# Where a selective scan takes its decay, its start state and its gate: four edits to one stage of a four-layer network

## The chip, the cores and the metric

The kernel runs on one core of a Trainium2 chip. The metric is device time in microseconds (us) for one execution of the whole program; three runs of the kernel before gave 5123.48, 5127.48 and 5133.85, median 5127.48 us. The engines are named as the profile names them: PE (matmuls), DVE (the vector engine), ACT (the scalar engine), POOL (GpSimd) and SP, whose queue issues nearly all DMAs. Each works through its own list of instructions in order, and semaphores make one wait for another. PSUM has eight banks of 128x512 f32 here, handed out by one pool.

## The reference, cut to what matters

Four layers of attention-like and feed-forward blocks run one after the other on a batch of 2. The change touches only the mixer of the third layer, a selective scan with 2048 channels and 16 states each over a sequence of 1024 (the kernel takes it over `S = 1024` as two halves of 512):

```python
def step(h, inp):
    x_t, dt_t, B_t, C_t = inp
    dA = jnp.exp(dt_t[..., None] * A)
    dBx = dt_t[..., None] * B_t[:, None, :] * x_t[..., None]
    h = dA * h + dBx
    y = jnp.einsum('bdn,bn->bd', h, C_t)
    return (h, y)
...
dt = jax.nn.softplus(dt + dt_bias[None, :, None])
...
y = (ys + D_param[None, :, None] * xc) * jax.nn.silu(z)
```

So each of 2048 x 16 rows needs a decay `dA` (an exponential), a term `dBx`, a recurrence along time, a product with `C`, a sum over the 16 states and a gate `silu(z)`.

## The kernel before, in words

`l2_attn` runs this stage once for each of the two batch entries. In it a loop over **slots** k does the scans; its order is written by hand (`manual_schedule`), so each engine's list is the order in which the loop emits. There are `SL = 128` slots for each half of the sequence (u = 0, then u = 1), so 256 a batch entry and 512 in all. Eight slots make a **chunk** of 128 channels; a slot holds 16 channels with 16 states, as two tiles (m = 0, 1) of 128 rows by 512 time steps.

What a slot k emits, in this order:

- `rows(k + 6)`: one DMA from DRAM (`dxd`) that spreads dt times x of the slot's channels over the states, into a tile `h` (nine buffers, 512 KB).
- `times_b(k + 2)`: POOL multiplies `h` by B (L1279, 128x1024).
- `keep(k - 1)`: in the first half only, ACT saves the last state of each row into `hst` in SBUF (L1304).
- `pe()`: one of two "calls", matmuls of other work that PE does alongside (input projections, gates, output projections of the first half).
- for m = 0 and 1: `scan(k, m)` on DVE (L1296; it reads the decay from PSUM and `h`, and writes `h`), then `decay(k + 1, m)`: a matmul on PE that spreads dt over the states into a PSUM bank (L1286), and ACT's exponential in place (L1288). In the second half ACT then adds the state carried over from the first half: `h[:, 0] += dA[:, 0] * hst`, a 128x1 operation (L1291); `scan` itself always starts from 0.0.
- between the two m: what has been put off to this slot with `at(...)`, and a second call.
- `states` in odd slots: matmuls that sum h times C over the states into a PSUM bank `py` (L1318; the first of a chunk is L1316).
- `times_c(k - 1)`: DVE multiplies `h` by C (L1307, 128x1024).

So DVE's own work in a plain slot is two scans and one L1307. Beside these stand, in the first half, three L1124 for each of 16 chunks (the conv's taps) and, in the second, additions to x and statistics (L152, L163).

**dt's chain.** `l2_dt` is called 16 slots before a chunk's first slot (call that slot k) and puts off the steps of softplus: relu, abs and exp on ACT at k+1 (`act1`), three more ACT operations at k+2 (`act2`, the last ones L1226 to L1228), two POOL operations at k+3 (`pool1`, L1231 and L1232), the sum at k+4 (L1235), dt times x at k+5 (`times_x`, L1238) with four DMAs to `dxd` (L1240), a rounded copy `hl` on ACT and its low part `lo` on POOL at k+7 (L1247, L1252), and two DMAs `hl<-lo` at k+8 (`send`, L1258). x itself (`xi`) is loaded at k+3. The chunk's `rows` begin at k+10, its decays at k+15. Tiles `e`, `one`, `lg` and `rl` have one buffer each.

**The gate.** `y_out` is put off to 8 slots after the chunk's fifth slot: ACT copies `py` from PSUM to a tile `one` (L1332), POOL multiplies the gate `zt` by it (L1333), SP writes the product to DRAM (L1334). `zt` holds silu(z), which `silu_z` makes in pairs on ACT, with a table load ahead and one behind (at L1129 and L193).

After the loop the second half's output projection reads these products back (`out_proj`, L1618 and L1622).

Of the kernel before, what the change touches and what calls it, by code (L numbers as in the profile page):

```python
# [11 lines left out]
AF = mybir.ActivationFunctionType  # L12
ALU = mybir.AluOpType
# [14 lines left out]
class Net:  # L28
# [1032 lines left out]
    def l2_attn(self, b, ready, last):  # L1061
        nc, i = self.nc, self.i
        NCH, N, NR = 16, 16, 64
        NF = NR + 2 * N
        SL = 8 * NCH
        with (
# [24 lines left out]
            hst = lp.tile([P, NCH * N], F, name=self.nm("hst"))  # L1091

            def tmp(tag, bufs=2, n=HALF):
                return tp.tile([P, n], F, tag=tag, bufs=bufs, name=self.nm(tag))
# [4 lines left out]
            xcd, yd = [dram(t, [P, HALF]) for t in ("xcd", "yd")]  # L1099
# [3 lines left out]
            px, norms, hl, hs, dA, py, xs = {}, {}, {}, {}, {}, {}, {}  # L1103
# [6 lines left out]
            def at(k, f, *args):  # L1110
                late.setdefault(k, []).append((f, args))
# [96 lines left out]
            def l2_dt(u, c, k):  # L1208

                p = self.ps()  # L1210
                nc.tensor.matmul(
                    p, wd[c // 8][: NF + 1, (c % 8) * P : (c % 8 + 1) * P], norms[u][0], start=True, stop=True
                )
                xs[u, c] = xc = tmp("xi")
                at(k + 3, nc.sync.dma_start, xc, xcd[u][c][:])
                e, one, lg = tmp("e", 1), tmp("one", 1), tmp("lg", 1)
                dt, dtx = lg, e
                rl = tmp("rl", 1)

                def act1():  # L1220
                    nc.scalar.activation(rl, p, AF.Relu)
                    nc.scalar.activation(e, p, AF.Abs)
                    nc.scalar.activation(e, e, AF.Exp, scale=-1.0)

                def act2():
                    nc.scalar.activation(one, e, AF.Identity, bias=self.one)  # L1226
                    nc.scalar.activation(lg, one, AF.Ln)
                    nc.scalar.activation(one, one, AF.Identity, bias=neg)  # L1228

                def pool1():  # L1230
                    nc.gpsimd.tensor_tensor(e, e, one, ALU.subtract)  # L1231
                    nc.gpsimd.tensor_tensor(lg, lg, e, ALU.add)  # L1232

                def sum1():
                    nc.gpsimd.tensor_tensor(dt, lg, rl, ALU.add)  # L1235

                def times_x():
                    nc.gpsimd.tensor_tensor(dtx, dt, xc, ALU.mult)  # L1238
                    for j in range(4):
                        nc.sync.dma_start(dxd[u][c][:, j, :], dtx[32 * j : 32 * j + 32, :])  # L1240

                low = [None]

                def parts():

                    hl[u, c] = tp.tile([P, 2, HALF], R, tag="hl", bufs=2, name=self.nm("hl"))
                    nc.scalar.copy(hl[u, c], dt.unsqueeze(1).to_broadcast([P, 2, HALF]))  # L1247

                def rest():

                    lo = low[0] = tp.tile([P, HALF], R, tag="lo", bufs=1, name=self.nm("lo"))
                    nc.gpsimd.tensor_tensor(lo, dt, hl[u, c][:, 0, :].bitcast(F), ALU.subtract)  # L1252

                def send():

                    lo = low[0]
                    for j in range(2):
                        nc.sync.dma_start(  # L1258
                            hl[u, c][64 - 64 * j : P - 64 * j, j, :].bitcast(F), lo[64 * j : 64 * j + 64, :].bitcast(F)
                        )  # L1260

                for n, f in ((1, act1), (2, act2), (3, pool1), (4, sum1), (5, times_x), (7, parts), (7, rest), (8, send)):
                    at(k + n, f)


# [17 lines left out]
            def decay(k, m):  # L1283
                u, c, q, jj = of(k)
                dA[k, m] = self.ps()
                nc.tensor.matmul(dA[k, m], rep[:, 4 * m + q, :], hl[u, c][:, jj, :], start=True, stop=True)  # L1286
                g = 16 * c + 4 * q + 2 * jj + m
                nc.scalar.activation(dA[k, m], dA[k, m], AF.Exp, scale=A[:, g : g + 1])  # L1288
                if u:
                    h0 = hs[k][:, m, 0:1]  # L1290
                    nc.scalar.activation(h0, dA[k, m][:, 0:1], AF.Identity, scale=hst[:, g : g + 1], bias=h0)  # L1291

            def scan(k, m):
                u, c, q, jj = of(k)
                g = 16 * c + 4 * q + 2 * jj + m
                nc.vector.tensor_tensor_scan(  # L1296
                    hs[k][:, m, :], dA.pop((k, m)), hs[k][:, m, :], 0.0, ALU.mult, ALU.add
                )

            def keep(k):  # L1300
# [27 lines left out]
            def y_out(k):  # L1328
                u, c = k // SL, k % SL // 8
                sz = zt.pop((u, c))  # L1330
                yo = tmp("one", 1)
                nc.scalar.copy(yo, py.pop((u, c)))  # L1332
                nc.gpsimd.tensor_tensor(sz, sz, yo, ALU.mult)  # L1333
                nc.sync.dma_start(yd[u][c][:], sz)  # L1334

            def ins(u):
# [125 lines left out]
            with self.tc.manual_schedule():  # L1462

                todo, ahead = [], []

                def take(units, lead):
                    for n, (load, calls) in enumerate(units):
                        ahead.append((len(todo) - lead, load))
                        todo.extend(calls)

                z0, z1, x1 = gates(0), gates(1), ins(1)
                take(z0[:2] + x1[:6], 20)
                for n in range(2, 12, 2):
                    take(z0[n : n + 2] + x1[n + 4 : n + 6], 20)
                take(xproj(1), 4)
                take(z0[12:] + z1[:6], 20)
                taken = 0
                at(-BEFORE, lambda: at(4 - BEFORE, l2_spread, 0, l2_norm(0)))
                for k in range(-BEFORE, 2 * SL + 6):
                    if -16 <= k < 2 * SL - 16 and k % 8 == 0:  # L1480
                        l2_dt((k + 16) // SL, (k + 16) % SL // 8, k)
                    if k == SL + 12:
                        o = outs(0)
                        for n, (a, z) in enumerate(((6, 10), (10, 12), (12, 16), (16, 16))):
                            take(o[8 * n : 8 * n + 8], 8)
                            take(z1[a:z], 20)
                    if k == -1 or k == SL:
                        l2_cr(max(k, 0) // SL)
                    n = 3 if k < -1 else 2
                    batch = []  # L1490
                    for _ in range(n):
                        while ahead and ahead[0][0] <= taken:
                            ahead.pop(0)[1]()
                        if taken < len(todo):
                            batch.append(todo[taken])
                            taken += 1

                    def pe(last=False):
                        while batch and (last or len(batch) > n - 1):
                            f, *args = batch.pop(0)  # L1500
                            if f:
                                f(*args, k)

                    live = 0 <= k < 2 * SL
                    if 0 <= k + 6 < 2 * SL:
                        rows(k + 6)
                    if 0 <= k + 2 < 2 * SL:
                        times_b(k + 2)
                    if 0 <= k - 1 < 2 * SL:
                        keep(k - 1)  # L1510
                    pe()
                    for m in range(2):
                        if live:
                            scan(k, m)
                        if 0 <= k + 1 < 2 * SL:
                            decay(k + 1, m)
                        if m:
                            break
                        for f, args in late.pop(k, []):
                            f(*args)  # L1520
                        pe(True)
                    if k % 2 == 1 and 0 <= k - 2 < 2 * SL:
                        states(k - 2)
                    if 0 <= k - 1 < 2 * SL:
                        times_c(k - 1)
                    if live and k % 8 == 4:
                        at(k + 8, y_out, k)
                    if live and k % 8 == 0:
                        skip(k // SL, k % SL // 8)
                while late:  # L1530
                    for f, args in late.pop(min(late)):
                        f(*args)
# [460 lines left out]
```

## Time and profile before

| | |
|---|---|
| three runs, median | 5127.48 us (5123.48 to 5133.85) |
| the profiled execution, its own time | 5130.32 us |
| its span in the profile | 5128.4 us |
| granted TensorE clock, mean | 0.968 |
| scan loop, first batch entry | 1052 to 2006 us |
| scan loop, second batch entry | 3602 to 4548 us |
| L1296, the scans | 1024 of 1207 ns mean |
| L1307, times C | 512 of 1193 ns mean |
| L1291, the state's addition on ACT | 512 of 352 ns mean |
| L1332, the copy for the gate on ACT | 64 of 585 ns median |
| L1333, the gate on POOL | 64 of about 1274 ns median |

The page gives, for each engine, busy time and the costliest groups of instructions with the idle time ahead of them and what ended it. The table of windows gives the same busy times for chosen stretches. A wait for several semaphores is put down to the one that came last. The two scan loops are 1900 us of the span; nothing outside them is touched by the change.

### The profile page before, as it was taken

The numbers are of one execution on the slowest core, as the hardware profiler recorded it, in microseconds if no ns is written. First come the engines' busy times: TensorE is split into PE (matmuls) and PEld (weight loads), VectorE is DVE, ScalarE is ACT, GpSimd is POOL, SyncE is SP. The second block draws the span as 40 slices with busy tenths as digits, with TensorE's granted clock in tenths as the row PEclk, the third lists the DMA queues.
The fourth block names the chain that finished last, engine by engine and source line by source line (L and its number), as shares of the span: only waits on it lengthen the run. The fifth ranks groups of instructions, "written<-read, shape, count | busy, mean of one in ns | idle before, by whom it ended". The sixth has DMA issues, their size and how long they took to land. (4 is left out here: it accounts for less than half of the span.)

```text
span 5128.4 us, 50257 instructions
## 1 busy us (share of the span) xinstructions
PE 4706.3 (92%) x16584; PEld 2237.2 (44%) x16584; DVE 3128.0 (61%) x4322; ACT 2109.7 (41%) x4485; POOL 2097.7 (41%) x1259
## 2 busy tenths in 40 slices
PE   8989989998897888999999999899888988899999
PEld 3347645433332333455433576554333333344544
DVE  5453256389999997225365422652899999963153
ACT  2431232377677774001024311424776777720010
POOL 2013121078798885100020220200887998831010
PEclk9999999999999999999999999999999999999999
DMA  2144212388889998201111432113888899971100
GB/s 88 36 159 143 97 48 81 131 216 217 220 225 242 236 244 226 90 33 46 49 67 38 173 119 89 54 51 103 220 219 224 214 247 245 249 210 65 55 20 33
DMA packets 254871, 708.06 MB, mean 138 GB/s; under 512 B 37008, under 2 KB 54544, under 8 KB 254612
## 3 DMA queue, kind: packets, MB, share of 16 engines
q1 hardware_dynamic: 248340, 683.88, 46.7%
q0 software_dynamic: 6272, 20.98, 1.2%
q8 instruction: 133, 2.18, 0.2%
q14 instruction: 126, 1.03, 0.1%
HBM read 599.60 MB, written 86.25 MB: 134 GB/s over the span
## 5 line engine op out<-in xcount | busy, mean ns | idle before, releaser
L1296 DVE TENSOR_TENSOR_SCAN h<-ps,h 128x512 f32<-128x512 f32 x1024 | 1204.1, 1207 | 88.9 <-ACT h L1291 47.2
L1279 POOL TENSOR_TENSOR h<-h,br 128x1024 f32<-128x1024 f32 x512 | 1201.0, 2367 | 43.3 <-DMA h<-dxd 20.7
L1286 PE MATMUL ps<-hl,rep 128*128 128x512 f32 x1024 | 717.9, 708 | 119.9 <-DVE h L1296 94.7
L1288 ACT ACTIVATE ps<-ps,l_Alog 128x512 f32<-128x512 f32 x1024 | 667.9, 657 | 216.9 <-PE ps L1286 213.6
L1307 DVE TENSOR_TENSOR h<-h,ps 128x1024 f32<-128x1024 f32 x512 | 610.8, 1193 | 0.0
L1403 PE MATMUL ps<-xT,w 128*128 128x512 f32 x1024 | 541.1, 615 | 10.2 <-DVE h L1296 7.9
L1608 POOL TENSOR_TENSOR x<-x,row 128x1024 f32<-128x1024 f32 x48 | 112.3, 2349 | 796.0 <-PE ps L130 796.0
L1286 PEld LDWEIGHTS ps<-hl,rep 128*128 128x128 f32 x1024 | 198.6, 195 | 523.6 <-DVE h L1296 340.1
L152 DVE TENSOR_TENSOR x<-x,ps 128x512 f32<-128x512 f32 x192 | 128.4, 681 | 434.4 <-PE ps L1785 145.6
L1318 PE MATMUL ps<-h,sel 128*32 128x512 f32 x2048 | 365.1, 638 | 18.8 <-DVE h L1307 18.2
L104 PE MATMUL ps<-xT,w 128*128 128x512 f32 x768 | 336.1, 592 | 0.0
L177 ACT ACTIVATE rs<-mv 128x1 f32<-128x1 f32 (+2 forms) x88 | 17.9, 203 | 705.7 <-DVE mv L171 705.4
L1441 PE MATMUL ps<-w,w 128*128 128x512 f32 x512 | 279.9, 630 | 20.8 <-DMA w<-yd 12.1
L1403 PEld LDWEIGHTS ps<-xT,w 128*128 128x128 f32 x1024 | 190.6, 195 | 204.2 <-issue 136.7
L104 PE MATMUL ps<-w,xT 128*128 128x512 f32 (+1 forms) x768 | 278.3, 522 | 0.0
L1124 DVE SCALAR_TENSOR_TENSOR ps<-xp,l_convw,ps 128x512 f32<-128x512 f32 x192 | 144.4, 752 | 213.4 <-ACT ps L1119 208.9
L767 POOL TENSOR_TENSOR s<-s,l1r 128x512 f32<-128x512 f32 x64 | 66.5, 1040 | 487.7 <-DVE l1r L766 481.8
L1349 PE MATMUL ps<-xT,w 128*128 128x512 f32 x512 | 251.9, 602 | 0.7
L1291 ACT ACTIVATE h<-ps,h,hst 128x1 f32<-128x1 f32 x512 | 180.0, 352 | 118.5 <-POOL h L1279 93.9
L1782 PE MATMUL ps<-w,xT 128*128 128x512 f32 x512 | 227.4, 597 | 0.0
L1622 PE MATMUL ps<-w,w 128*128 128x512 f32 x512 | 222.6, 594 | 4.2 <-DMA w<-yd 4.2
L104 PEld LDWEIGHTS ps<-xT,w 128*128 128x128 f32 x768 | 144.8, 189 | 183.4 <-issue 177.6
(289 smaller groups left out, 7319.9 us busy)
## 6 DMA issues: line engine op xcount, KB each, us to landing
h<-dxd SPq DMA_DIRECT2D x512, 512.0 KB, 7.2
w<-l_in SPq DMA_DIRECT2D x128, 512.0 KB, 6.7
w<-l_out SPq DMA_DIRECT2D x96, 512.0 KB, 6.2
w<-l_conv SPq DMA_DIRECT2D x54, 512.0 KB, 3.9
w<-cvd SPq DMA_DIRECT2D x36, 512.0 KB, 3.3
w<-l_fw SPq DMA_DIRECT2D x32, 512.0 KB, 4.4
xcd<-xo SPq DMA_DIRECT2D x64, 256.0 KB, 2.2
xi<-xcd SPq DMA_DIRECT2D x64, 256.0 KB, 5.4
```

What stands on the lines that cost most here:

```text
L104: self.nc.tensor.matmul(out, lhsT, rhs, start=j == 0, stop=j == n - 1)
L1279: nc.gpsimd.tensor_tensor(hs[k], hs[k], norms[of(k)[0]][1].unsqueeze(1).to_broadcast([P, 2, HALF]), ALU.mult)
L1286: nc.tensor.matmul(dA[k, m], rep[:, 4 * m + q, :], hl[u, c][:, jj, :], start=True, stop=True)
L1288: nc.scalar.activation(dA[k, m], dA[k, m], AF.Exp, scale=A[:, g : g + 1])
L1296: nc.vector.tensor_tensor_scan(hs[k][:, m, :], dA.pop((k, m)), hs[k][:, m, :], 0.0, ALU.mult, ALU.add)
L1307: nc.vector.tensor_tensor(hs[k], hs[k], norms[of(k)[0]][3].unsqueeze(1).to_broadcast([P, 2, HALF]), ALU.mult)
L1318: nc.tensor.matmul(py[u, c][32 * j : 32 * j + 32, :], self.sel[:, q, :], hs[k - 1 + j // 2][:, j % 2, :], start=False, stop=q == 3,)
L1349: nc.tensor.matmul(p, w["w"][:, k * P : (k + 1) * P], self.xcols(k, u0, HALF), start=k == 0, stop=k == KD - 1)
L1403: nc.tensor.matmul(p, w["w"][:, k * P : (k + 1) * P], self.xcols(k, u * HALF, HALF), start=k == 0, stop=k == KD - 1)
L1441: nc.tensor.matmul(p, y[:, cc, t * P : (t + 1) * P], wt[:, cc * HALF : (cc + 1) * HALF], start=c2 == 0 and cc == 0, stop=last,)
L1622: nc.tensor.matmul(acc[tt], y[:, cc * HALF + tt * P : cc * HALF + (tt + 1) * P], w[:, cc * HALF : (cc + 1) * HALF], start=c == 0, stop=c = ...
L1782: nc.tensor.matmul(p, self.xcols(k, tt * P, P), wt[k][:, ns], start=k == 0, stop=False)
```

## The change

Four edits, all in `l2_attn`:

1. `decay` is emitted for the tiles (k+1, 1) and (k+2, 0) in slot k, where it was (k+1, 0) and (k+1, 1).
2. dt's chain is spread: its ACT steps stand in slots k+1 to k+5, its POOL steps in k+5 and k+6, the sum in k+7, `times_x` with its four DMAs and the rounded copy in k+8, the low part in k+9, `send` in k+10; x is loaded at k+4. dt times x goes to the tile `one` and no longer to `e`.
3. The ACT operation L1291 is gone; in the second half `scan` takes `hst[:, g : g + 1]`, one value a partition in SBUF, as its start, and 0.0 in the first.
4. `y_out` comes 6 slots after the chunk's fifth slot, not 8; one DVE operation multiplies the gate by `py` in PSUM, in place of ACT's copy and POOL's product.

```diff
-                at(k + 3, nc.sync.dma_start, xc, xcd[u][c][:])
+                at(k + 4, nc.sync.dma_start, xc, xcd[u][c][:])
-                dt, dtx = lg, e
+                dt, dtx = lg, one
...
-                for n, f in ((1, act1), (2, act2), (3, pool1), (4, sum1), (5, times_x), (7, parts), (7, rest), (8, send)):
+                for n, f in (
+                    (1, act1), (2, act2), (3, act3), (4, act4), (5, act5), (5, pool1), (6, pool2), (7, sum1),
+                    (8, times_x), (8, parts), (9, rest), (10, send),
+                ):
                     at(k + n, f)
...
                 nc.scalar.activation(dA[k, m], dA[k, m], AF.Exp, scale=A[:, g : g + 1])
-                if u:
-                    h0 = hs[k][:, m, 0:1]
-                    nc.scalar.activation(h0, dA[k, m][:, 0:1], AF.Identity, scale=hst[:, g : g + 1], bias=h0)
...
-                    hs[k][:, m, :], dA.pop((k, m)), hs[k][:, m, :], 0.0, ALU.mult, ALU.add
+                    hs[k][:, m, :], dA.pop((k, m)), hs[k][:, m, :], hst[:, g : g + 1] if u else 0.0, ALU.mult, ALU.add
...
-                yo = tmp("one", 1)
-                nc.scalar.copy(yo, py.pop((u, c)))
-                nc.gpsimd.tensor_tensor(sz, sz, yo, ALU.mult)
+                nc.vector.tensor_tensor(sz, sz, py.pop((u, c)), ALU.mult)
                 nc.sync.dma_start(yd[u][c][:], sz)
...
-                        if 0 <= k + 1 < 2 * SL:
-                            decay(k + 1, m)
+                        if 0 <= k + 1 + m < 2 * SL:
+                            decay(k + 1 + m, 1 - m)
...
-                        at(k + 8, y_out, k)
+                        at(k + 6, y_out, k)
```

In the new chain `act1` holds relu and abs, `act2` the exponential, `act3` the addition of one, `act4` the logarithm, `act5` the subtraction of one, `pool1` and `pool2` one POOL operation each. The instructions are otherwise the same, in the same number.

More of the change, by code (lines that the diff above doesn't have):

```diff
@@ L1222, in act1, with act2, act3, act4 @@
                     nc.scalar.activation(e, p, AF.Abs)
+                def act2():
                     nc.scalar.activation(e, e, AF.Exp, scale=-1.0)
-                def act2():
+                def act3():
                     nc.scalar.activation(one, e, AF.Identity, bias=self.one)
+                def act4():
                     nc.scalar.activation(lg, one, AF.Ln)
+                def act5():
                     nc.scalar.activation(one, one, AF.Identity, bias=neg)
@@ L1231, in pool1, with pool2 @@
                     nc.gpsimd.tensor_tensor(e, e, one, ALU.subtract)
+                def pool2():
                     nc.gpsimd.tensor_tensor(lg, lg, e, ALU.add)
```

## The prediction

> **What bounds it now.** I read the page's busy shares first, then the table of windows for the four halves of the two scan loops, then DVE's waits there, then the timeline around the long ones. Over the whole span PE is the busiest engine, but the change touches only the scan loops, so their rows decide.
>
> ```profile
> 1052.00:1536.00 484.00, 428.38 (x1341) 162.61 (x1339) 462.52 (x437) 344.63 (x658) 418.51 (x226) 0.97 0.83 220
> 1536.00:2006.00 470.00, 396.70 (x1244) 148.14 (x1242) 443.18 (x401) 339.86 (x675) 399.98 (x212) 0.95 0.93 241
> 3602.00:4084.00 482.00, 428.81 (x1340) 162.89 (x1339) 462.79 (x437) 344.60 (x659) 418.83 (x226) 0.97 0.83 220
> 4084.00:4548.00 464.00, 398.17 (x1247) 147.26 (x1245) 442.39 (x401) 339.76 (x674) 399.90 (x212) 0.95 0.93 245
> ```
>
> Columns: length, then PE, PEld, DVE, ACT, POOL busy, clock, DMA share, GB/s. DVE is busy 1810.9 of 1900 us: it sets the loops' pace, and 89.1 us of idle is all that better feeding can win. PE's modelled 85-89% is no second bound: in the timeline a call starts 0.43 us after the one before and a decay adds about 0.23, with four state sums near 0.5, so some 1.8 us of a 3.36 us slot. POOL's 85% and the DMAs' 93% in second halves are nearer.
>
> ```profile
> DVE h L1296 <- ACT h L1291: 26.1, 33, 2.3
> DVE h L1296 <- ACT ps L1288: 13.2, 14, 2.3
> DVE h L1296 <- DMA dxd<-e: 5.7, 1, 5.7
> DVE ss L1176 <- ACT pn L1171: 2.5, 1, 2.5
> ```
>
> These are DVE's waits in the first loop (us, times, longest). L1291 exists in second halves only: 26.1 here and 21.1 in the second loop are all of their idle. What stands behind one such wait:
>
> ```profile
> 1766.93 1.28 POOL L1238 TENSOR_TENSOR e<-lg,xi 128x512 f32<-128x512 f32 x1 [5.18 <-DMA xi<-xcd]
> ...
> 1770.55 0.35 ACT L1291 ACTIVATE h<-ps,h,hst 128x1 f32<-128x1 f32 x1 [3.37 <-POOL h L1279]
> ...
> 1770.93 1.22 DVE L1296 TENSOR_TENSOR_SCAN h<-ps,h 128x512 f32<-128x512 f32 x1 [2.28 <-ACT h L1291]
> ```
>
> x's load came late, POOL stood 5.18 us, its next product was late, ACT's queue stood behind L1291, and DVE lost 2.28. In the first half it is ACT's own burst: two table loads and three silus fill 1101.46 to 1105.69, the next decay's exponential waits behind them, and DVE loses 2.32 us at 1106.40.
>
> **What it adds to DVE.** In a plain stretch slots start 3.36 us apart, while two scans (1.211) and L1307 (1.194) last 3.616: each starts some 0.085 before its forerunner ends. So an operation occupies DVE for its duration less 0.085.
>
> ```profile
> L152 DVE TENSOR_TENSOR x<-x,ps x192: 632/686/691, 179.7 to 5120.3; 128x512 f32<-128x512 f32 x192
> L628 DVE SCALAR_TENSOR_TENSOR qkv<-cf,ps x22: 677/689/690, 380.5 to 3141.5; 128x512 f32<-128x512 f32 x22
> L1723 DVE SCALAR_TENSOR_TENSOR x<-ps,rinv,x x32: 740/745/752, 2368.3 to 4978.9; 128x512 f32<-128x512 f32 x32
> ```
>
> - Gate: L152 is its form (SBUF times PSUM into SBUF, min/median/max ns). 64 x (0.686 - 0.085) = **38.5 us**. The Trainium skill's VectorE: DVE Perf Modes, The DRAIN you can't avoid, has the next operation wait until the pipe is empty: 64 x 0.686 = 43.9; it also says that one that isn't held starts earlier, and slots of 3.36 show by how much: I take 38.5. Its new wait is for PE's last state sum. Behind it in DVE's list stand scan (k, 1) and all that follows. The latest that PE starts on it is when a scan frees a bank, two operations and 2.24 us ahead; PE needs one decay and eight sums (0.5 + 1.07), so it is on time by some 0.6 us.
> - Start state: no scan with a start from SBUF is in the trace. L628 has a constant as its scalar and 689 ns, L1723 one value a partition and 745; L1124, of L1723's kind, has 756. So 0 (the fetch is hidden, and an added fetch can't shorten a scan) to 0.070 a scan; nearest is L1723 against L628, 0.056, say 0.058 with L152 beside it: 512 x 0.058 = **29.7**, between 0 and 36.
>
> Sum: 68.2 us more on the engine that bounds.
>
> **What it takes away.** 512 L1291 (180 us of ACT), 64 L1332 (37) and 64 L1333 (82 of POOL): all beside DVE, worth only the waits. From the 89.1 idle I keep 9.9 (first loop) and 10.9 (second): first scan 5.7, first taps 1.2, the norm's chain 3.0 and 4.0. The rest is 68.3; each of about 92 stalls also loses its 0.085 overlap, so 76 is to be had.
>
> - POOL in eight slots: 8 x 2.367 + 6 x 1.273 = 26.6 us against eight slots of DVE at 26.9 to 29. Without the gate 25.3: it can run ahead again.
> - x's load moves one slot later but its user three: in the median 7.4 us lie between load and use now, and two slots (6.7 us) more then. The 5.18 us wait goes. SP passes it in the slot after the one whose `states` free its buffer, so SP stands less.
> - ACT's burst now has one exponential ahead of it and the next is due 1.5 slots later. ACT's chain steps come singly.
> - The gate's DMA moves two slots up; it waits for one DVE operation, not for ACT and POOL in turn.
>
> I count 72 of the 76: DVE's inputs then come with more than a slot to spare. The first scan gains too: before the loop a slot is PE's 2.68 us ((1031.13 - 1009.66) / 8) and its first decay comes one slot up: 2 us each, 4 in all. The tail: L1622 stands 1.72 us for a load that SP issues behind the gate's write; 3 in all.
>
> **What gets tighter** (times from slot starts). The four `dxd` writes move three slots: the last is issued 6.1 us (median) after its slot starts, lands 2.9 later, so 9 us after slot k+8's start; `rows` stands in SP's list at k+10, 6.7 us after. SP is held about 2 us a chunk with weights and rows behind it; now POOL's first product of a chunk starts 11.6 us or more after its DMA is issued, which lands in 7.2. Hidden. `act3` must await the old `dxd` writes as `one` is their source: three slots, 10 us, against 9, and ACT may be 5 late before DVE is. `send`:
>
> ```profile
> L1258 SPq EVENT_SEMAPHORE  x64: 17/17/17, 1026.6 to 4492.9; - x64
> ...
> DMA to landing us min/median/max: 2.3/8.6/11.7
> ```
>
> Issued about 1.5 us after its slot's start, plus 1 behind `rows`: landed 11 us after slot k+10's start. PE asks for it at k+14.3 (14.6 us), DVE misses it after some 18.4. Hidden by 7 in the median. Before, DVE's slack was 14.
>
> **Sum:** 68.2 - 72 - 4 - 3 = -11 against the profiled execution's own 5130.3, so 5119; less 11 from the runs' median, 5116. Every term is read or worked out from that one trace, which is 0.06% above the median.
>
> **The rule that speaks against it.** The Trainium skill's Perfetto Trace Analysis, Optimizing Scalar/DVE Operations, advises to move work off a saturated DVE to ScalarE or GpSimd; this goes the other way. By the rule alone DVE is 95% busy in the loops, so +68 (5196). The rows have 89 us of idle that come from just those helpers. I follow the rows, but they leave only 11.
>
> **Rivals.**
>
> - The start state is free (18%): for it, DVE has the scan's other operands to fetch anyway; against it, L1723, and L1183, which at 128x16 takes 226 ns where L1758 with a constant takes 175 at 128x15. Then -11 - 30 = -41: 5086.
> - `hl` comes late (30%), the other side: PE's list stops at a chunk's first decay, with states and calls behind it. For it: slack halved to 7 us, landings to 11.7, sends as late as 8.5, DMAs at 93%. Against: the median. It decides from 18.4 us after slot k+10's start; 0.6 us a chunk over 62 chunks is 37, so -11 + 37 = +26: 5153.
> - "Sooner" is not sooner (10%): a decay needs a bank, and in both lists most take the one freed by the scan four before (173 of 256 in a first half, 121 after; 104 and 107 in a second). If banks, not order, time the exponentials, the first halves' 29 stay: -11 + 27 = +16, 5143. Against it: the burst on ACT is order.
>
> **Numbers.** Forecast case 42%, with its own -25 to +3. About 0.2% (10 us) is what a measurement tells from no change: of this case 0.22 is faster, 0.20 same. The free start adds 0.18 faster; `hl` 0.28 slower and 0.02 same; banks 0.08 slower, 0.02 same. Faster 0.40, same 0.24, slower 0.36. The range runs from 5084 to 5153, from free start to late `hl`.
>
> **What would show it.** Scans of second halves near 1.27 us against 1.21 in first halves (free: equal). 64 new DVE rows of 0.69. DVE idle in both loops near 25, no L1291. POOL busy 82 less. PE's waits for `hl<-lo` near zero; if they run to tens of us, the second rival. I am wrong if DVE's idle stays above 40, or if the gate waits for PE at most chunks.

## The result, and the profile after

The change makes the kernel slower: 5152.3 us in the median of 6 runs (5146.4 to 5156.8) against 5130.7 for the kernel before in 6 runs beside them; ratio 1.0040, 95% interval 1.0027 to 1.0054. The forecast was 11 us faster. The profiled execution has a span of 5149.7 us (before 5128.4).

The table of windows of the kernel after, again one row for each half of the two scan loops (length, then PE, PEld, DVE, ACT and POOL busy, clock, DMA share, GB/s):

```profile
1052.00:1545.00 493.00, 420.77 (x1344) 158.72 (x1342) 471.45 (x452) 333.50 (x646) 399.02 (x211) 0.97 0.80 215
1545.00:2021.00 476.00, 405.51 (x1269) 146.83 (x1268) 470.27 (x430) 250.60 (x404) 383.05 (x201) 0.95 0.91 244
3611.00:4103.00 492.00, 421.14 (x1336) 158.57 (x1335) 469.48 (x451) 330.91 (x640) 396.56 (x210) 0.96 0.80 214
4103.00:4571.00 468.00, 402.31 (x1246) 145.96 (x1245) 464.37 (x417) 250.51 (x402) 382.03 (x198) 0.93 0.91 245
```

ACT and POOL lost the work that was taken from them (in each second half ACT is busy 89 us less, POOL 17), and in the second halves DVE hardly stops: 470 of 476 and 464 of 468. The first halves are another matter: 493 and 492 long, with DVE still idle for over 20 us each. These windows are cut at round times, so from here on I measure a half from the start of its first scan to that of the next half (or to its last scan), with DVE's idle time in brackets, added up over the two batch entries:

| | first halves, us (DVE idle) | second halves, us (DVE idle) |
|---|---|---|
| before | 966.6 (40.6) | 925.8 (48.4) |
| after | 988.0 (44.8) | 925.6 (5.3) |

So the whole loss of 21 us is in the first halves: the gates add 17 us of work to DVE there, and its idle time, 29 us of which was to go, grew by 4. The second halves did what was forecast, to no gain: 43 us of stalls went, and as much work came. Two views price that work: the page's groups for the scans and for times C (L1304 and L1315 here; form, count, busy us, mean ns, idle ahead of them) and the gate's line alone (min, median, max ns).

```profile
L1304 DVE TENSOR_TENSOR_SCAN h<-ps,hst,h 128x512 f32<-128x512 f32 x512 | 629.8, 1262 | 1.5 <-issue 1.3
L1315 DVE TENSOR_TENSOR h<-h,ps 128x1024 f32<-128x1024 f32 x512 | 610.1, 1192 | 31.0 <-ACT hst L1312 29.6
L1304 DVE TENSOR_TENSOR_SCAN h<-ps,h 128x512 f32<-128x512 f32 x512 | 601.1, 1206 | 11.4 <-ACT ps L1299 11.4
```

```profile
L1339 DVE TENSOR_TENSOR row<-row,ps x32: 650/659/689, 1090.2 to 4520.9; 128x512 f32<-128x512 f32 x32
L1339 DVE TENSOR_TENSOR zo<-zo,ps x32: 648/657/687, 1152.7 to 4573.8; 128x512 f32<-128x512 f32 x32
its engine sat idle before it (us, times) until:
  PE ps L1326: 4.3, 5
```

A scan that takes its start state from SBUF lasts 1262 ns against 1206. The gate takes 658 ns and waits for PE five times, 4.3 us in all. The second row of the first fence is the news: times C stood 29.6 us for L1312, which is `keep`, ACT's copy of the end state. Before the change it waited for nothing (the last number of its row there is 0.0):

```profile
L1307 DVE TENSOR_TENSOR h<-h,ps 128x1024 f32<-128x1024 f32 x512 | 610.8, 1193 | 0.0
```

DVE's waits in the first batch entry's first half (us in total, times, longest):

```profile
DVE h L1315 <- ACT hst L1312: 13.8, 6, 3.1
DVE h L1304 <- ACT ps L1299: 5.7, 1, 5.7
DVE ss L1176 <- ACT pn L1171: 4.1, 1, 4.1
...
ACT ps L1299 <- PE ps L1297: 85.9, 88, 3.6
```

The last line is ACT's own: its exponentials (L1299) stood 85.9 us for the decays' matmuls, about twice as long as in the same half before:

```profile
ACT ps L1288 <- PE ps L1286: 43.5, 57, 4.0
```

One of the six waits of times C, in the timeline (start, duration, instruction, idle ahead of it):

```profile
1114.58 2.33 DVE L1304 TENSOR_TENSOR_SCAN h<-ps,h 128x512 f32<-128x512 f32 x2
...
1115.85 0.29 PEld L1297 LDWEIGHTS ps<-hl,rep 128*128 128x128 f32 x1 [0.88 <-DVE h L1304]
1115.85 1.12 PE L1297 MATMUL ps<-hl,rep 128*128 128x512 f32 x1
...
1117.01 0.66 ACT L1299 ACTIVATE ps<-ps,l_Alog 128x512 f32<-128x512 f32 x1 [3.19 <-PE ps L1297]
1117.60 1.04 ACT L1255 CAST hl<-lg 128x1024 fp32r<-128x1024 f32 x1
1118.65 1.28 ACT L1129 ACT_TABLE_LOAD   x1
1119.95 0.60 ACT L1129 ACTIVATE xo<-ps 128x512 f32<-128x512 f32 x1
1120.56 1.28 ACT L193 ACT_TABLE_LOAD   x1
1121.86 0.66 ACT L1299 ACTIVATE ps<-ps,l_Alog 128x512 f32<-128x512 f32 x1
1122.44 0.39 ACT L1334 ACTIVATE dg<-ident,l_D 128x128 f32<-128x128 f32 x1
1122.73 0.18 ACT L1312 COPY hst<-h 128x2 f32<-128x2 f32 x1
...
1122.94 1.22 DVE L1315 TENSOR_TENSOR h<-h,ps 128x1024 f32<-128x1024 f32 x1 [2.68 <-ACT hst L1312]
```

Read it from below. Times C overwrites the tile whose last column `keep` must first save, so it waits for `keep`. `keep` took its turn in ACT's list behind a rounded copy, a burst of two table loads with a silu, and two exponentials. All of these were late because ACT had stood 3.19 us at one exponential. Its matmul (1115.85) began when the first of the two scans above it had ended, at 1115.79; that scan freed the bank that this decay writes. Before the change ACT stood at exponentials for half as long, and times C never had to wait for `keep`.

### The profile page after: what moved, and what is told of

It is laid out like the page before. It is cut to its first block, busy times and chain, and to the rows that moved or that the text cites. A ratio compares the mean times of both kernels' runs of the same rounds, so it can differ in the third digit from the quotient of the medians.

```text
span 5149.7 us, 49145 instructions
## 1 busy us (share of the span) xinstructions
PE 4693.5 (91%) x16584; PEld 2219.5 (43%) x16584; DVE 3188.4 (62%) x4386; ACT 1906.0 (37%) x3909; POOL 2015.7 (39%) x1195
## 5 line engine op out<-in xcount | busy, mean ns | idle before, releaser
L1290 POOL TENSOR_TENSOR h<-h,br 128x1024 f32<-128x1024 f32 x512 | 1204.6, 2369 | 79.8 <-DMA h<-dxd 63.0
L1299 ACT ACTIVATE ps<-ps,l_Alog 128x512 f32<-128x512 f32 x1024 | 674.3, 662 | 579.8 <-PE ps L1297 575.4
L1297 PE MATMUL ps<-hl,rep 128*128 128x512 f32 x1024 | 683.2, 673 | 200.9 <-DVE h L1304 168.8
L1304 DVE TENSOR_TENSOR_SCAN h<-ps,hst,h 128x512 f32<-128x512 f32 x512 | 629.8, 1262 | 1.5 <-issue 1.3
L1315 DVE TENSOR_TENSOR h<-h,ps 128x1024 f32<-128x1024 f32 x512 | 610.1, 1192 | 31.0 <-ACT hst L1312 29.6
L1304 DVE TENSOR_TENSOR_SCAN h<-ps,h 128x512 f32<-128x512 f32 x512 | 601.1, 1206 | 11.4 <-ACT ps L1299 11.4
L1326 PE MATMUL ps<-h,sel 128*32 128x512 f32 x2048 | 323.5, 643 | 8.1 <-DVE h L1315 8.1
L1447 PE MATMUL ps<-w,w 128*128 128x512 f32 x512 | 275.1, 621 | 5.7 <-DVE h L1304 5.7
L1237 POOL TENSOR_TENSOR e<-e,one 128x512 f32<-128x512 f32 x64 | 81.5, 1273 | 485.3 <-ACT one L1234 402.5
```

The costliest lines, as they stand in the source:

```text
L1290: nc.gpsimd.tensor_tensor(hs[k], hs[k], norms[of(k)[0]][1].unsqueeze(1).to_broadcast([P, 2, HALF]), ALU.mult)
L1304: nc.vector.tensor_tensor_scan(hs[k][:, m, :], dA.pop((k, m)), hs[k][:, m, :], hst[:, g : g + 1] if u else 0.0, ALU.mult, ALU.add)
L1315: nc.vector.tensor_tensor(hs[k], hs[k], norms[of(k)[0]][3].unsqueeze(1).to_broadcast([P, 2, HALF]), ALU.mult)
L1326: nc.tensor.matmul(py[u, c][32 * j : 32 * j + 32, :], self.sel[:, q, :], hs[k - 1 + j // 2][:, j % 2, :], start=False, stop=q == 3,)
L1447: nc.tensor.matmul(p, y[:, cc, t * P : (t + 1) * P], wt[:, cc * HALF : (cc + 1) * HALF], start=c2 == 0 and cc == 0, stop=last,)
```

## The experiments

Fourteen kernels were run, each timed beside the kernel before on the same chip (whose median was 5126.9 to 5131.1 in these sets, so the ratio is what compares). The table gathers them; the halves are those of one profiled execution each, measured as above.

| kernel | ratio, 95% interval | first halves (idle) | second halves (idle) |
|---|---|---|---|
| edit 1 alone | 1.0106, 1.0087 to 1.0126 | 1013.4 (85.5) | 934.9 (59.0) |
| edit 2 alone | 0.9956, 0.9940 to 0.9972 | 962.5 (37.4) | 902.9 (30.8) |
| edit 3 alone | 0.9984, 0.9973 to 0.9995 | 966.4 (40.5) | 908.9 (7.6) |
| edit 4 alone | 0.9971, 0.9960 to 0.9983 | 967.8 (24.2) | 921.4 (29.0) |
| edits 2, 3, 4 | 1.0024, 1.0014 to 1.0034 | 968.0 (26.8) | 925.9 (5.9) |
| all, `keep` first | 1.0027, 1.0016 to 1.0038 | 978.5 (36.5) | 923.8 (3.7) |
| edit 1, `keep` first | 1.0107, 1.0085 to 1.0128 | 1011.2 (84.0) | 933.7 (57.5) |
| edit 1, matmuls only | 1.0011, 0.9997 to 1.0025 | 961.1 (39.9) | 930.9 (54.6) |
| all, of edit 1 matmuls only | 1.0006, 0.9996 to 1.0015 | 966.8 (27.2) | 924.7 (4.3) |
| before, one bank fewer | 1.0246, 1.0229 to 1.0263 | 1045.6 (116.9) | 955.6 (74.9) |
| before, one bank more | 1.0575, 1.0558 to 1.0593 | 1106.5 (79.5) | 1074.6 (90.7) |
| edit 1, one bank more | 1.0565, 1.0545 to 1.0586 | 1115.6 (69.3) | 1064.1 (77.0) |
| edits 2 and 3 | 0.9992, 0.9982 to 1.0001 | 965.4 (38.9) | 918.7 (16.1) |
| edits 2 and 4 | 0.9979, 0.9969 to 0.9988 | 972.5 (29.5) | 910.8 (20.5) |

### Each edit by itself

The waits of the kernel after allow two theories. Theory ONE: the rounded copy of dt, moved by edit 2 into the slot of ACT's burst, makes `keep` late, and the decays' shift (edit 1) is innocent. Theory TWO: the shift itself does it. Each edit was made alone; for edit 2 alone the gate's copy gets a tile of its own, since dt times x now lives in `one`.

Edit 1 alone:

```diff
-                        if 0 <= k + 1 < 2 * SL:
-                            decay(k + 1, m)
+                        if 0 <= k + 1 + m < 2 * SL:
+                            decay(k + 1 + m, 1 - m)
```

> The kernel before with the first edit alone (decays half a slot sooner). Theory ONE says that in the changed kernel's first halves the vector engine waits for ACT's saved state because the rounded copy of dt (now eight slots on) falls into the slot of the silu burst, so ACT reaches keep too late; the decays' shift is innocent. Then this kernel loses the 29 us of waits for exponentials that first halves have, gets no waits of times C for keep (under 4 us), and leaves second halves as they are: about -25 us against before. Theory TWO says the shift itself puts one more exponential ahead of keep behind the burst: waits of L1307's operation for keep of 20 to 30 us appear here too, and the time is within 8 us of before.

Edit 2 alone (the chain as in the change, and):

```diff
-                yo = tmp("one", 1)
+                yo = tmp("yo", 1)
```

> The kernel before with the second edit alone (dt's chain spread; the gate's copy gets a tile of its own name). Theory ONE: the rounded copy now stands in the burst's slot, ahead of the second exponential: first halves get longer waits, each of six burst slots by about 1 us, 10 to 25 us more in all, second halves little changed (within 8 us). Theory TWO: no harm, first halves equal or up to 10 us shorter.

Edit 3 alone:

```diff
-                if u:
-                    h0 = hs[k][:, m, 0:1]
-                    nc.scalar.activation(h0, dA[k, m][:, 0:1], AF.Identity, scale=hst[:, g : g + 1], bias=h0)
...
-                    hs[k][:, m, :], dA.pop((k, m)), hs[k][:, m, :], 0.0, ALU.mult, ALU.add
+                    hs[k][:, m, :], dA.pop((k, m)), hs[k][:, m, :], hst[:, g : g + 1] if u else 0.0, ALU.mult, ALU.add
```

> The kernel before with the third edit alone (scan starts from the state in SBUF, no ACT operation for it). If the second halves' waits are from ACT's queue standing behind that operation: their 48 us of idle fall below 10, scans of second halves take 0.05 us longer (26 us in all), first halves stay: about -17 us against before. If the waits need POOL's relief (the gate moved off it) to go: idle stays near 30 to 40 as waits for POOL, and the time is 5 to 20 us above before.

Edit 4 alone:

```diff
-                yo = tmp("one", 1)
-                nc.scalar.copy(yo, py.pop((u, c)))
-                nc.gpsimd.tensor_tensor(sz, sz, yo, ALU.mult)
+                nc.vector.tensor_tensor(sz, sz, py.pop((u, c)), ALU.mult)
...
-                        at(k + 8, y_out, k)
+                        at(k + 6, y_out, k)
```

> The kernel before with the fourth edit alone (gate on the vector engine from PSUM, two slots sooner). The vector engine gets 64 operations of 0.66 us (36 us occupied). If the gate on ACT and POOL was behind the second halves' waits, these fall by 20 or more and the time is within 20 us above before; if not, the time is 30 to 36 us above before with the same waits.

Measured: 5188.6 us for edit 1 alone, 5107.7 for edit 2, 5121.3 for edit 3, 5120.0 for edit 4, against 5130.9: **+58, -23, -10, -11**. Theory ONE fell at once: the shift is the only edit that does harm, and by itself it does nearly three times the harm of the whole change. Theory TWO had the waits for `keep` right (20 to 30 us in a half; 30.5), the time not: it had it within 8 us of before. Edit 4 came out better than either of its forecasts, which both had a loss: DVE got 33 us of work in the loops and lost 36 of idle. The waits of edit 1 alone in its first half (here L1307 is times C, L1304 `keep`, L1288 the exponential and L1286 the decay's matmul, as in the kernel before):

```profile
DVE h L1307 <- ACT hst L1304: 30.5, 14, 4.3
DVE h L1296 <- ACT ps L1288: 7.1, 7, 4.8
...
ACT ps L1288 <- PE ps L1286: 122.2, 103, 5.4
```

They have the same two names as in the kernel after: times C waits for `keep`, and ACT waits for PE's decays, now 122 us of one half. How much sooner did the decays come? From the trace, the median time between the end of an exponential and the start of its scan was 3.13 us (m = 0) and 2.36 us (m = 1) in the first halves before. Emitting it half a slot (1.7 us) sooner raised that to only 3.62 and 2.84.

### Without the shift, and with `keep` out of its way

If the shift alone is bad, leaving it out should give 5130.9 - 44. And if it is bad because `keep` stands behind one more exponential, putting `keep` ahead of that should cure it. The first kernel is the change without edit 1. The others have this, on edit 1 alone and on all four edits:

```diff
-                    if 0 <= k - 1 < 2 * SL:
-                        keep(k - 1)
...
                             scan(k, m)
+                            if m:
+                                keep(k)
```

> Edits 2, 3 and 4 together, without the decays' shift (keep then stands where it stood before the change). Theory THREE: the shift alone is the harm, and the other three add up: 5130.9 - 23 - 10 - 11 = about 5087, ratio 0.9915, first halves near 482 us and second halves near 450. In the first halves no wait of VectorE for hst above that of before. Rival FOUR: the edits need each other (the gate's place on VectorE needs decays that come sooner, or state and gate gain the same stalls twice): 5100 to 5115, and VectorE waits for the exponential in the second halves more than 10 us.

> The decays' shift alone, with keep (the end state's copy on ScalarE) put right behind the scan that makes it, ahead of the exponential that is now emitted sooner. Rival FIVE (order of keep): the shift hurts because times C waits for keep, which stands behind one more exponential: the 30.5 us of waits for hst in the first half go and the time is back at before or below it, 5115 to 5135. Theory THREE in its narrow form (banks): the exponential itself waits for a decay matmul that waits for a bank freed by the scan four earlier, and holds all that is queued behind it on ScalarE; then the waits for hst go but waits for other ScalarE results (ps, h) come in their place, ScalarE still waits more than 90 us for PE's decays in the first half (43.5 in the kernel before, 122 with the shift alone), and the time stays at 5155 to 5185.

> All four edits, with keep put right behind the scan that makes it. Rival FIVE (order of keep): the 29.7 us of waits for hst in the two first halves go, nothing takes their place, and the time falls to about 5125 or below, ratio 0.996 to 1.000 against the kernel before. Theory THREE (banks): the waits change their name and the time stays at 5140 to 5155.

Edits 2, 3 and 4 together took 5139.4 us against 5126.9, 12 us slower than before and not 44 faster: Theory THREE was wrong about the sum, and rival FOUR was right that they don't add up, though not about how far, nor about the waits (in the first batch entry's second half DVE waits 2.6 us for exponentials, where it had over 10). Without edit 1 the first halves are back at 968.0, 20 us less than after, and the second halves are the same as after. Against before, the profiled execution is only 1.5 us longer in the loops; 6.9 more lie outside them, on which more below. Moving `keep` did nothing for edit 1 alone (5184.2; waits for `keep` in its first half still 24.5 us) and in the full change gave back about half of the first halves' 20 us (978.5; 5141.0 us in all), with 9.6 us of waits for `keep` still in the first of them. Rival FIVE fell as the whole account. In its new place `keep` still stands behind the other exponential of its slot, and with edit 1 alone ACT still stood 99.6 us for the decays.

### TensorE's side or ScalarE's side of the shift

The shift moves two instructions for each decay: the matmul in PE's list, which also takes the bank half a slot sooner, and the exponential in ACT's. They can be moved apart. These kernels move only the matmul:

```diff
                 nc.tensor.matmul(dA[k, m], rep[:, 4 * m + q, :], hl[u, c][:, jj, :], start=True, stop=True)
+
+            def exps(k, m):
+                u, c, q, jj = of(k)
                 g = 16 * c + 4 * q + 2 * jj + m
                 nc.scalar.activation(dA[k, m], dA[k, m], AF.Exp, scale=A[:, g : g + 1])
...
-                        if 0 <= k + 1 < 2 * SL:
-                            decay(k + 1, m)
+                        if 0 <= k + 1 + m < 2 * SL:
+                            decay(k + 1 + m, 1 - m)
+                        if 0 <= k + 1 < 2 * SL:
+                            exps(k + 1, m)
```

> Only half of edit 1: the decays' matmuls half a slot sooner, their exponentials (and the second halves' start state) left at their old place in ScalarE's order. If the harm of the shift comes from TensorE's side (banks held half a slot longer, TensorE's queue standing for a bank that a scan has still to free), it is all here: 5160 to 5190, like the 5188.6 of the shift alone. If it comes from ScalarE's order (keep and the conv burst behind one more exponential), it is gone: 5120 to 5140, and TensorE's waits for scans in the first half stay near the 38 us of the kernel before.

> All four edits, but of edit 1 only the matmuls come half a slot sooner; the exponentials keep their old place in ScalarE's order (the start state is the scan's operand, as in the change). ScalarE's order as the cause: the first halves' waits for hst go and their length falls from 493 and 495 to about 484, as without edit 1 (483 and 485); time 5133 to 5142, ratio about 1.002. If in the full change it is the banks held longer or TensorE's order, the first halves stay at 490 or more and the time at 5148 to 5156.

With the matmuls alone moved, the kernel before becomes 5135.2 us (ratio 1.0011, no change that can be told) where the full shift cost 58. In the full change the same edit gives 5134.2 us (1.0006), 3.4 thousandths of the time or 17 us less than after, and the first halves fall from 988.0 to 966.8. Their waits in the first of them (ACT's lines after the dots; here the scan is L1307, the exponential L1302, `keep` L1315):

```profile
DVE h L1307 <- ACT ps L1302: 10.6, 7, 5.7
DVE ss L1176 <- ACT pn L1171: 4.5, 1, 4.5
...
ACT hst L1315 <- DVE h L1307: 46.7, 36, 3.7
ACT hst L1315 <- POOL lg L1243: 31.5, 10, 4.3
ACT hst L1315 <- issue: 19.6, 14, 6.1
ACT hst L1315 <- POOL h L1290: 13.1, 6, 3.7
ACT ps L1302 <- PE ps L1297: 12.7, 14, 3.8
```

Nothing of DVE waits for `keep` any more. And ACT's idle time has changed place: it stands 12.7 us at exponentials, not 85.9, and now mostly at `keep`, for a scan that has still to end, with everything else done. That is the harm of the shift in one comparison. ACT works its list in order; with the exponential early in the list, ACT stands at it, and what it could have done meanwhile (table loads, silus, copies out of PSUM, `keep`) comes late.

One thing blurs the comparison: moving instructions also changes which bank the pool hands to which decay. In the full change this is small. The decays that take a bank freed by the scan three or four before are 142 of 256 in a first half with the whole shift and 122 with the matmuls alone, and at the decays PE stood nearly alike for scans (35.3 and 32.0 us in the first of them), while ACT's wait fell from 85.9 to 12.7. With edit 1 alone it is larger (187 against 154), so a part of its 58 us may be that; the two were not separated. Nor was it tested why the shift makes the loops 56 us longer by itself and only 20 on top of the other three edits.

### Why the early exponential isn't ready: the banks

Its matmul can't run until a bank is free, and many decays take the bank that the scan four before frees: 173 of 256 in a first half before, 155 with edit 1 alone, 121 in the whole change. For (k + 2, 0) that is scan (k, 0), in the slot in which the shift emits it. The order in which the pool hands out the banks can be laid beside the traces of both first halves. Before, the scan that frees the bank had always ended by the time that ACT came to an exponential at which it then stood. With edit 1 alone it had not at 24 of them (80 of 251 us of such waits), in the whole change at 37 (63 of 170 us). At the rest the bank was free by then but the matmul not yet done, or the bank came from something else than a scan.

Two kernels change the number of banks. One holds a second copy of C in PSUM through each half:

```diff
                 nc.scalar.copy(norms[u][3], norms[u][2])
+                norms[u][4] = self.ps()
+                nc.scalar.copy(norms[u][4], norms[u][2])
```

and reads two columns of it at the half's end. The other reads C from SBUF, which frees a bank, drops the copy of C into PSUM and gives C's tile in SBUF a second buffer. It was made of the kernel before and of edit 1 alone:

```diff
-                    hs[k], hs[k], norms[of(k)[0]][3].unsqueeze(1).to_broadcast([P, 2, HALF]), ALU.mult
+                    hs[k], hs[k], norms[of(k)[0]][2].unsqueeze(1).to_broadcast([P, 2, HALF]), ALU.mult
```

> The kernel before with one PSUM bank fewer to rotate through in the loop (a second copy of C is held there; it costs one copy on ScalarE per half and moves no other instruction): most decays then wait for the scan three earlier instead of four, the same distance in scans that the shift leaves between a decay's place and the scan that frees its bank. Bank theory: it costs what the shift costs, 5165 to 5200. If banks don't matter at this distance: 5125 to 5140.

> The decays' shift alone, with C's broadcast left in SBUF instead of PSUM, so that the pool of PSUM tiles that the decays rotate through has one bank more and most decay matmuls wait for the scan five earlier instead of four. Theory THREE (banks): ScalarE's waits for PE's decays in the first half fall from 122 us to below 70, VectorE's waits for hst fall below 15, and the time is 5120 to 5145. Rival FIVE (order of keep): waits for hst stay at 20 to 30 in the first half and the time at 5175 to 5190. Reading C from SBUF instead of PSUM may itself change the multiplication's duration on VectorE; its row tells by how much.

> The kernel before with C read from SBUF (one PSUM bank more), the control of the run with the shift and that bank (5417.7). Times C from SBUF took 1642 instead of 1193 ns there, 512 x 0.449 = 230 us. If the extra bank cures the shift, this control is near 5415 too (its own stalls hidden or not, between 5340 and 5420); if it doesn't, this control is near 5127 + 230 = 5357 and the shift still costs 57 on top.

One bank fewer costs the kernel before 124 us (5253.5 against 5129.5), twice what the shift costs and more than was expected of it. ACT's waits in its first half look like the shift's; DVE then waits for the exponentials themselves and not for `keep` (exponential L1290, decay matmul L1288; up to 1540 us, 37 us short of the half's end):

```profile
DVE h L1298 <- ACT ps L1290: 43.4, 21, 5.7
...
ACT ps L1290 <- PE ps L1288: 126.6, 108, 6.2
```

ACT stands 126.6 us for decays without any exponential having been moved. With one bank more the shift costs nothing that can be told: 5417.7 with it (ratio 1.0565), 5427.0 without (1.0575), and with it ACT stands 64.1 us for decays in the first half where it was 122.2, times C 7.8 us for `keep` where it was 30.5. Both of these kernels are far slower for another reason, below, and their slots are longer. Their first halves still differ by 9 us to the shift's disadvantage, their second by 10 the other way. So this last pair says less than the first: it agrees with the banks as the cause, and is not proof by itself.

### Why the three good edits don't add up

> Edits 2 and 3. Additive: 5130.9 - 23 - 10 = 5098. Shared stalls (each edit takes from the same 24 us of VectorE's stalls per second half, which can be taken once): edit 2 left 15 of it, edit 3 adds 14 us of scan time per second half and finds no more than 13 to take, so the time is that of edit 2 alone, 5104 to 5112, the second halves 450 to 453 us long with 1 to 4 us of idle.

> Edits 2 and 4. Additive: 5130 - 23 - 11 = 5096. Shared stalls: edit 2 alone left 19 us of VectorE's idle in a first half and 15 in a second; edit 4 adds 9 us of work to each and, alone, took 9 out of the idle of each: if it finds them again the halves stay at 482 and 451 and the time at 5104 to 5112 (that of edit 2 alone); if edit 2 and edit 4 free the same stalls, the halves are 487 to 491 and 456 to 460 and the time is 5120 to 5135.

Edits 2 and 3 together: 5126.0 us (-3.5), above both forecasts; edits 2 and 4: 5124.3 us (-7), as forecast for stalls that both edits free. Neither pair is better than edit 2 alone. The idle columns of the table say why. Before, DVE stood idle for 89.0 us in the loops. Alone, edit 2 takes 20.8 of that, edit 3 40.9 and edit 4 35.8: together 97.5, more than there is. With all three (and the matmuls' part of edit 1) 57.5 are gone, so 40 us of the single gains were the same stalls counted twice. The work that edits 3 and 4 add to DVE, in contrast, adds up in full: its busy time in the loops rises by 24 us with edit 3, by 33 with edit 4 and by 58 with edits 2, 3 and 4. In the second halves DVE then is idle for 4.3 of 924.7 us: those halves can't become shorter by feeding it better.

Sharing doesn't explain the pairs wholly. Edits 2 and 3 leave 16.1 us of idle in the second halves where edit 3 alone leaves 7.6, with DVE's waits again for exponentials (9.9 us in the first of them); which step of dt's chain stands ahead of those was not tried. The spans outside the loops also differ from profile to profile by up to 18 us (3233 to 3251) in single executions. They go with the clock that PE was granted: between the two loops it was 0.978 in the 1595.0 us of edit 2 alone and 0.980 in the 1596.3 of edit 4 alone, 0.975 in the 1599.7 before, 0.972 in the 1604.1 of edits 2, 3 and 4, and 0.970 in the 1608.3 of edits 2 and 3. Whether an edit in the loops sets that clock was not tested.

The best kernel that was run is edit 2 alone: 5107.7 us, ratio 0.9956 (0.9940 to 0.9972), faster than the kernel before and the kernel after. It adds no work to DVE.

## Why the prediction was wrong

- **The cost on DVE was right.** Forecast 38.5 + 29.7 = 68.2. The 62 gates inside the loops each occupied 0.58 us (36), and a scan with a start state 1.186 us, against 1.129 for one without in the second halves of the kernel with edit 2 alone, over the second halves' 510 scans 29: 65. So the rival of a free start state is out.
- **The second halves were right.** DVE's idle there fell from 48.4 to 5.3 us. The wait for x's load and the wait for L1291 are gone, as the four steps about POOL, x's load and the gate's write had it.
- **The first halves were wrong, and decide it.** The step that failed is "I count 72 of the 76: DVE's inputs then come with more than a slot to spare", and in it "ACT's burst now has one exponential ahead of it and the next is due 1.5 slots later". Of the first halves' 29 us nothing came; their idle rose from 40.6 to 44.8, 33 us away from the forecast, which is nearly the whole miss (11 forecast gain, 21 measured loss). Over all loops 39 us of idle went, where 72 were forecast; the 50 that stayed are above the 40 that the prediction named as a sign of being wrong. I looked at which exponential DVE would wait for behind the burst and moved that ahead. That part is true: in the whole change the median lead of an exponential over its scan rose to 4.51 and 4.27 us, and DVE waits for one only once in a half. I did not ask what would then stand behind that exponential in ACT's list, nor when its bank comes. `keep`, due within half a slot, is the answer; the forecast doesn't name it.
- **The rival "sooner is not sooner"** had +16 and 10%, and is the nearest in its mechanism. It put the cause on the banks *instead of* the order. The runs say both: the order of ACT's list does the harm (in the full change 988.0 us of first halves with the whole shift, 966.8 with its matmuls alone), and at 37 of the exponentials at which ACT then stands the bank isn't free when their turn comes, at none before. I had counted how many decays wait for the scan four before, and argued it away with the burst. ("Most" was right for a first half before, 173 of 256, but not for the other three counts, 121, 104 and 107.)
- **The rival `hl` late** did not happen, though its 5153 is nearest of all to the measured 5152.3; that is chance. PE waited for the load of `hl` once, for 0.2 us, and the gate's waits for PE are 4.3 us over all 64.
- **Two small terms failed.** The first scans did not start sooner (1052.2 against 1052.1, and in the second entry 1601.6 us after the first entry's last scan against 1599.7), where 4 us were counted. The tail gained 2 of 3 (584.2 to 582.3 from the last scan).
- **The rule of the Trainium skill** (Perfetto Trace Analysis, Optimizing Scalar/DVE Operations: offloading work from a saturated DVE may make sense) would have had +68 where the rows gave -11. Edit 4 alone, which puts work on DVE, gave -11: busy for 95% of the loops, DVE still had stalls that this edit took away. Put beside edits 2 and 3, which leave less idle, the same edit brings 32 us of work and takes only 22 of idle (loops of 1893.9 us with it, 1884.1 without). The sum of the three, each a gain, is 58 us of work against 56 of idle. Edit 2 is the one that feeds DVE better and gives it no work.

## What to carry to other kernels

When an instruction is moved up in an engine's list, ask when its inputs and its buffer can be ready at the new place, and list what stands behind it that was done by then at the old one; an early place for an operation that isn't ready is a stop for all of it. Here moving the producer without its consumer did no harm that can be told (1.0011), nor any good. And add up gains only after checking that they don't come from the same idle time: stalls can be taken once, while the work that pays for them is added every time.

## What the runs showed of the hardware

C read from SBUF and not from PSUM made times C slower on DVE by a third, and POOL's products with it. The first row is the line in the kernel before (min, median, max ns), the second in the kernel before with C in SBUF:

```profile
L1307 DVE TENSOR_TENSOR h<-h,ps x512: 1183/1194/1211, 1060.1 to 4547.7; 128x1024 f32<-128x1024 f32 x171
```

```profile
L1307 DVE TENSOR_TENSOR h<-h,cr x512: 1192/1274/3260, 1063.3 to 4844.1; 128x1024 f32<-128x1024 f32 x171
```

The shortest are nearly equal and the longest nearly three times as long; the mean is 1599 ns, and 512 x 0.406 = 208 of the 297 us that this kernel loses. POOL is the other party. The 15 of these 512 beside which POOL worked for less than a twentieth of their time took 1192 to 1216 ns. POOL's 128x1024 products rose from 2367 to 2986 ns in the mean, but took 2352 where no times C ran beside them and 3349 where two did. The Trainium skill's GPSIMD Engine Reference says so in its table of the engine (SBUF shared with VectorE, contention with instructions of two SBUF inputs); here is its price. So the copy of C into PSUM, which takes a bank that the decays are short of, is worth having.
